# Overflow guard of three attentions: bounds from the weights' Gram matrices in place of peaks of the queries and keys

## The chip, the cores and the metric

The kernel is one program on one core of one Trainium2 chip. The core has five engines with queues of their own: TensorE (PE; its weight loads are listed as PEld), VectorE (DVE), ScalarE (ACT), GpSimd (POOL) and SyncE (SP, which here only issues transfers). The metric is the device time of one execution in microseconds (us); lower is better. A profile is one execution taken by the hardware profiler, and its span runs from the first to the last instruction.

## What is computed

A chain of 16 layers on 4096 tokens of 128 features (16 sequences of 256 tokens), all in float32. Three layers matter here; all are attentions whose softmax the kernel works out without subtracting a row maximum. `x` below is the layer-normed input of the layer.

```
# decay (16 heads of 8)
q = x @ Wq.T + bq;  k = x @ Wk.T + bk
scores = (q . k) * 8**-0.5 * exp(-alpha * |i - j|)
attn = softmax(scores)

# window and sink (16 query heads of 64, 4 key heads)
x = rmsnorm(x, attn_norm_scale)
q = rope(x @ Wq + bq) * 64**-0.25;  k = rope(x @ Wk + bk) * 64**-0.25
scores = where(|i - j| <= 128, q . k, -1e9)
attn = softmax([scores, sink])[..., :-1]

# rope (16 heads of 8; only the real parts are kept)
Q[even] = cos * (x @ Wq + bq)[even] - sin * (x @ Wq + bq)[odd];  K alike
attn = softmax(causal(Q . K / 8**0.5))
```

## The kernel before

The program holds two networks. `Fast` computes every layer and, in softmax, takes exp of the raw scores. That is safe only while no score is large, so `Fast` keeps a table `peaks` of magnitudes, and at its end `over` (L2733) reduces the table to one number for each stage and side (queries, keys), multiplies the two sides, and compares the product with `LIMITS` (L43). If a limit is exceeded, a branch runs `Net`, the same network with row maxima, over everything again. `bad` is a second condition of decay: a negative `alpha`.

Before the change the table is filled with `peak` (L1666): a VectorE `tensor_reduce` that takes the largest magnitude of each partition over one chunk of queries or keys. The tokens are worked in eight chunks of 512 (two sequences).

Decay and rope run in `small_stage` (L2797). Its loop over slots writes every engine's order out by hand: a slot takes one unit of scores (a 128x128 tile of all 16 heads, four matmuls into four PSUM banks), whose exponentials are evicted by ScalarE, or in decay, for the tiles near the diagonal, first multiplied by the decay factors on VectorE (`pt<-ps,dec`). Products with the values follow three slots later, then a copy `raw` of the sums, transposes (`ct,raw`), division, output projection. Banks are of one pool of six, handed out in turn, so a matmul waits for whoever reads the bank of six allocations ago. A list `steps` gives the slot, relative to a chunk's first unit, at which a chunk's other work is issued: projections, masked copies of the queries, and `guard`, at slot 1. In decay a chunk is eight slots; in rope six, with scores taken three units at a time. The steps of the next layer's beginning (`lead`) run beside them; behind decay that is the router of a mixture of experts (`both`, `rank`, `sel`, `idx`), which is mostly small VectorE operations.

Window and sink attention (L3160) has a schedule of its own: 128 units, one a slot; query and key projections in `prepare` at every second slot, their rotation by VectorE (products with cos and sin, a shuffle) and POOL (the sum), peaks four slots later at the end of the slot, the sums of two units' probabilities on POOL (`both`), and four banks for scores and projections.

The rows of the profile name operations by helper: L504 is every matmul (`mm`), L508 every transpose, L528 every ScalarE activation, L531 and L543 VectorE's products, L534 POOL's.

Of the kernel before, what the change touches and what calls it, by code (L numbers as in the profile page):

```python
# [39 lines left out]
BOUND, LOW = 60.0, 38.0  # L40
PEAKS = 4 * NCH
STAGES = DECAY, ROPE, WINDOW, WINDOW1, SINKS, LOCAL_A, LOCAL_B = range(7)
LIMITS = (BOUND * 8**0.5 / 8, BOUND * 8**0.5 / 4, LOW / 64, LOW / 64, LOW, LOW / 8, LOW / 8)  # L43


class Pack:
# [1603 lines left out]
class Fast(Net):  # L1650
# [15 lines left out]
    def peak(self, stage, side, n, ap):  # L1666

        at = (stage * 2 + side) * PEAKS + n
        self.nc.vector.tensor_reduce(self.peaks[:, at : at + 1], ap, AX.XY if len(ap.shape) > 2 else AX.X, ALU.max, apply_absolute_value=True)

    def weights(self, st):

        self.wpool = self.pool(st, "weights", 1)
        self.turns = 0
        self.widths = [max([1] + [self.packs[n].n for n in self.loads[i::2]]) for i in range(2)]
# [1276 lines left out]
    def decay(self, w):  # L2952


        h0 = self.ha
        nc = self.nc
        with ExitStack() as st:
            p1 = self.stage(st, "d1", 1)
            p2 = self.stage(st, "d2", 2)
            na = p1.tile([P, 1], F32, tag="na", name="na")  # L2960
            self.ts(na, w["alpha"], -1.0, ALU.mult)
            dec = p1.tile([P, P], F32, tag="dec", name="dec")
            self.act(dec, w["lag"][:, :P], AF.Exp, scale=na)
            edge = p1.tile([P, T], F32, tag="edge", name="edge")
            self.act(edge, w["edge"], AF.Exp, scale=na)
            bad = p1.tile([P, 1], F32, tag="bad", name="bad")
            self.ts(bad, w["alpha"], 0.0, ALU.is_lt, 1e30, ALU.mult)
            vzs = self.with_ones(p1, 2)

            def evict(kind, pt, ps):  # L2970
                if kind:
                    for r in range(4):
                        self.act(pt[:, r].rearrange("p h t -> p (h t)"), ps[r], AF.Exp, scale=8.0**-0.5)
                    return
                for r in range(4):
                    self.tt(pt[:, r], ps[r].rearrange("p (h t) -> p h t", h=4), dec[:, None, :].broadcast_to([P, 4, P]), ALU.mult)
                flat = pt.rearrange("p r h t -> p (r h t)")
                return lambda: self.act(flat, flat, AF.Exp, scale=8.0**-0.5)

            qs, ks, kxs, qzs, qxs = {}, {}, {}, {}, {}  # L2980

            def project(c):
                for n, held in (("q", qs), ("k", ks)):
                    pq = self.bank("s")
                    self.mm(pq, w["W" + n], h0[:, self.chunk(c)])
                    held[c] = p2.tile([P, CH], F32, tag=n, name=n)
                    self.act(held[c], pq, AF.Identity, bias=w["b" + n])

            def values(c):
                self.values_by_head(w, vzs[c % 2], self.chunk(c))  # L2990

            def queries(c, b):
                qzs[c, b] = self.masked_copy(p1, qs[c], b)

            def keys_by_edge(c):
                kxs[c] = p2.tile([P, CH], F32, tag="kx", name="kx")
                self.gt(self.bt(kxs[c]), self.bt(ks[c]), self.twice(edge), ALU.mult)

            def queries_by_edge(c, b):
                qxs[c, b] = p1.tile([P, 4, T], F32, tag="qx", name="qx", bufs=3)  # L3000
                self.gt(qxs[c, b], qzs[c, b], edge[:, None, :].broadcast_to([P, 4, T]), ALU.mult)

            def guard(c):
                self.guard(DECAY, c, qs[c], ks[c])
                if c == 0:
                    at = DECAY * 2 * PEAKS
                    self.tt(self.peaks[:, at : at + 1], self.peaks[:, at : at + 1], bad, ALU.add)

            def tiles(c, b, it, jt):
                kk, qq = (ks, qzs) if it == jt else (kxs, qxs)  # L3010
                j = b * T + jt * P
                return kk[c][:, j : j + P], qq[c, b][:, :, it * P : it * P + P], vzs[c % 2][:, 2 * b + jt]

            steps = [
                (1, guard), (-6, project), (-5, values), (-4, lambda c: queries(c, 0)), (-3, keys_by_edge),
                (-2, lambda c: queries_by_edge(c, 0)), (0, lambda c: queries(c, 1)), (2, lambda c: queries_by_edge(c, 1)),
            ]
            units = [(0, 0, 0), (0, 1, 1), (1, 1, 0), (1, 0, 1)]
            self.small_stage(w, units, steps, tiles, evict)

    def guard(self, stage, c, q, k):
        self.peak(stage, 0, c, q)
        self.peak(stage, 1, c, k)

    def rope(self, w):
        h0 = self.ha
        nc = self.nc
        with ExitStack() as st:
            p1 = self.stage(st, "o1", 1)
            p2 = self.stage(st, "o2", 2)  # L3030
            vzs = self.with_ones(p1, 2)

            def evict(kind, pt, ps):
                for r in range(4):
                    self.act(pt[:, r].rearrange("p h t -> p (h t)"), ps[r], AF.Exp, scale=8.0**-0.5)
                if kind:
                    p = pt.rearrange("p r h t -> p (r h) t")
                    return lambda: self.tt(p, p, w["causal"][:, None, :].broadcast_to([P, 16, P]), ALU.mult)

            held, qzs = {}, {}  # L3040

            def turned(c, n):
                s = self.chunk(c)
                pe, po = self.bank("s"), self.bank("s")
                self.mm(pe, w[f"W{n}e"], h0[:, s])
                self.mm(po, w[f"W{n}o"], h0[:, s])
                t1 = p2.tile([P, CH], F32, tag=n, name=n)
                t2 = p2.tile([P, CH], F32, tag="t2", name="t2")
                self.stt(self.bt(t1), self.bt(pe), w[f"b{n}e"], self.twice(w["cos"]), ALU.add, ALU.mult)
                self.stt(self.bt(t2), self.bt(po), w[f"b{n}o"], self.twice(w["sin"]), ALU.add, ALU.mult)  # L3050
                self.gt(t1, t1, t2, ALU.subtract)
                held[c, n] = t1

            def values(c):
                self.values_by_head(w, vzs[c % 2], self.chunk(c))

            def queries(c, b):
                qzs[c, b] = self.masked_copy(p1, held[c, "q"], b)

            def tiles(c, b, it, jt):  # L3060
                j = b * T + jt * P
                return held[c, "k"][:, j : j + P], qzs[c, b][:, :, it * P : it * P + P], vzs[c % 2][:, 2 * b + jt]

            steps = [
                (-6, lambda c: turned(c, "q")), (-5, lambda c: turned(c, "k")), (-3, values), (-2, lambda c: queries(c, 0)),
                (0, lambda c: queries(c, 1)), (1, lambda c: self.guard(ROPE, c, held[c, "q"], held[c, "k"])),
            ]
            units = [(0, 0, 1), (1, 0, 0), (1, 1, 1)]
            self.small_stage(w, units, steps, tiles, evict, group=3)
# [90 lines left out]
    def window_attention(self, w, h, n1, ns2):  # L3160
# [3 lines left out]
        with ExitStack() as st:  # L3164
# [28 lines left out]
            def later(slot, f, *args):  # L3193
                due.setdefault(slot, []).append((f, args))

            def prepare(i, step, slot):

                c, side = divmod(i, 2)
                s = self.chunk(c)
                while pending:  # L3200
                    moved()
                if step == 0:
                    qs[i] = p2.tile([P, 4, CH], F32, tag="q", name="q")
                    ks[i] = p2.tile([P, CH], F32, tag="k", name="k")
                    roped("k", side, s, ks[i])
                    later(("last", slot + 4), self.peak, WINDOW + side, 1, c, ks[i])
                for g in ((0,), (1, 2), (3,), ())[step]:
                    roped("q", 4 * side + g, s, qs[i][:, g])
                    later(("last", slot + 4), self.peak, WINDOW + side, 0, 4 * c + g, qs[i][:, g])
                if side == 0 and step > 1:  # L3210
                    pv = self.bank("s")
                    v = p1.tile([P, 2, T], F32, tag="v", name="v", bufs=4)
                    for k in range(2):
                        t = 2 * step - 4 + k
                        self.mm(pv[:, k * T : k * T + T], n1[:, c * CH + t * P : c * CH + t * P + P], w["Wv"])
                        vs[c, t] = v[:, k]
                    self.tt(v, self.bt(pv), w["bv"][:, None, :].broadcast_to([P, 2, T]), ALU.add)
# [626 lines left out]
```

## Time and profile before

| what | us |
|---|---|
| timed runs: lowest, median, highest of 3 | 4231.14, 4233.71, 4234.19 |
| the profiled execution | 4216.97 |
| its span | 4215.2 |
| one peak of 128x512 on VectorE (median of 80 / of 32) | 0.676 / 0.671 |
| their sum (112 of them) | 74.2 |
| stretch of decay, with the end of the layer before | 2160 to 2440 |
| stretch of window and sink attention, without its start | 2900 to 3340 |
| stretch of rope | 3640 to 3840 |

In the timelines a row has the start (us from the start of the span), the time it covers (us), engine, line, operation, tiles written and read, shape, and the count of instructions merged into it; in brackets the idle time of the engine before it and what ended it. A float32 matmul has two records, so `x8` of a full matmul is four matmuls. Rows of one engine can overlap a little, since operations are pipelined.

### The profile page before, as it was taken

How to read it: one execution, taken by the hardware profiler on the slowest of the kernel's cores; microseconds unless marked ns; L12 is line 12 of the kernel's file. 1: busy time of each engine (PE TensorE's matmuls, PEld its weight loads, DVE VectorE, ACT ScalarE, POOL GpSimd, SP SyncE). 2: the span in 40 equal slices, each digit the busy share in tenths (PEclk: the TensorE clock that was granted, in tenths of full speed). 3: DMA queues.
4: the chain of work that ended last, by engine and by line, in shares of the span. 5: the costliest groups of instructions: out<-in, count | busy, mean ns of one | idle time of the engine just before them, and what ended most of it. 6: DMA issues, size and time to landing. Idle time of an engine off the chain costs nothing. (4 is left out here: it accounts for less than half of the span.)

```text
span 4215.2 us, 73089 instructions
## 1 busy us (share of the span) xinstructions
PE 3849.9 (91%) x28742; PEld 2195.1 (52%) x28742; DVE 2557.5 (61%) x4503; ACT 2314.2 (55%) x4485; POOL 1854.9 (44%) x1632
## 2 busy tenths in 40 slices
PE   7999999988899999985989879888999999899878
PEld 3555466465465456554965469543444344455333
DVE  4775576364577377464346633556877677486474
ACT  6666466555766466553456634444555554774532
POOL 4764365232566176326433434454555454321251
PEclk8999999988999999997999979999999999999989
DMA  1800000000000000004920058100000000000000
GB/s 61 345 2 1 11 2 1 20 1 1 20 1 1 3 1 1 1 6 142 320 76 12 16 180 297 41 19 16 1 1 1 3 1 10 6 2 19 6 0 21
DMA packets 78400, 176.38 MB, mean 42 GB/s; under 512 B 12606, under 2 KB 39108, under 8 KB 77920
## 3 DMA queue, kind: packets, MB, share of 16 engines
q1 hardware_dynamic: 65568, 148.40, 10.2%
q0 software_dynamic: 9120, 18.51, 1.3%
q8 instruction: 229, 3.75, 0.4%
q10 hardware_dynamic: 3360, 4.72, 0.4%
q14 instruction: 123, 1.01, 0.1%
HBM read 118.28 MB, written 54.20 MB: 41 GB/s over the span
## 5 line engine op out<-in xcount | busy, mean ns | idle before, releaser
L528 ACT ACTIVATE pt<-ps 128x512 f32<-128x512 f32 x640 | 339.9, 600 | 327.6 <-PE ps L504 326.4
L504 PE MATMUL ps<-hb,w 128*128 128x512 f32 (+1 forms) x960 | 461.0, 613 | 3.7 <-issue 3.3
L504 PE MATMUL ps<-w,hb 128*128 128x512 f32 (+2 forms) x896 | 403.8, 572 | 23.5 <-DVE t L531 18.6
L534 POOL TENSOR_TENSOR t<-t,t 128x512 f32<-128x512 f32 x256 | 319.8, 1271 | 161.1 <-DVE t L531 140.6
L531 DVE TENSOR_TENSOR t<-ps,tab 128x512 f32<-128x512 f32 x512 | 317.7, 682 | 84.6 <-ACT sq L528 81.1
L534 POOL TENSOR_TENSOR t<-t,ss 128x1024 f32<-128x1024 f32 x128 | 243.7, 1904 | 192.8 <-ACT ss L528 191.6
L504 PEld LDWEIGHTS ps<-hb,w 128*128 128x128 f32 (+1 forms) x960 | 178.6, 190 | 259.6 <-issue 223.0
L528 ACT ACTIVATE qkt<-ps 128x512 f32<-128x512 f32 x256 | 140.5, 595 | 291.7 <-PE ps L508 291.7
L531 DVE TENSOR_TENSOR u<-u,ps 128x384 f32<-128x384 f32 (+1 forms) x206 | 121.8, 596 | 288.0 <-PE ps L508 186.4
L531 DVE TENSOR_TENSOR ot<-ps,rd 128x512 f32<-128x512 f32 (+2 forms) x224 | 143.3, 640 | 203.2 <-ACT rd L528 203.2
L534 POOL TENSOR_TENSOR nsq<-ha 128x512 f32<-128x512 f32 x112 | 123.5, 1103 | 320.6 <-ACT ha L528 308.6
L504 PEld LDWEIGHTS ps<-w,hb 128*128 128x128 f32 x896 | 157.1, 194 | 178.6 <-issue 125.5
L534 POOL TENSOR_TENSOR both<-pt 128x1024 f32<-128x1024 f32 x64 | 151.2, 2363 | 199.8 <-DVE pt L531 164.1
L504 PE MATMUL ps<-nsq,ct 128*128 128x512 f32 x368 | 203.1, 635 | 34.3 <-POOL nsq L534 30.4
L504 PE MATMUL ps<-ot,w 128*128 128x512 f32 x448 | 213.2, 610 | 17.7 <-DVE ot L531 9.8
L504 PE MATMUL ps<-xt,w 128*128 128x128 f32 x1704 | 221.3, 281 | 1.5 <-ACT xt L528 1.5
L2199 POOL DMA_INDIRECT back<-y,x x142 | 139.1, 980 | 184.1 <-DVE y L538 63.3
L504 PE MATMUL ps<-u,w 128*128 128x512 f32 (+1 forms) x448 | 215.4, 605 | 3.5 <-POOL u L534 3.5
L504 PEld LDWEIGHTS ps<-xt,w 128*128 128x128 f32 x1704 | 205.2, 195 | 2.9 <-ACT xt L528 2.9
L528 ACT ACTIVATE u<-ps,w 128x512 f32<-128x512 f32 x160 | 107.8, 685 | 179.6 <-PE ps L504 177.0
L528 ACT ACTIVATE nrs<-ps,ct 128x512 f32<-128x512 f32 x208 | 139.7, 683 | 103.4 <-PE ps L504 97.8
L3741 POOL DMA_INDIRECT rows<-out,idx x128 | 126.1, 985 | 155.0 <-ACT out L528 105.5
(362 smaller groups left out, 8880.2 us busy)
## 6 DMA issues: line engine op xcount, KB each, us to landing
w<-in_moe_x SPq DMA_DIRECT2D x142, 533.0 KB
rows<-t SPq DMA_DIRECT2D x64, 520.0 KB
x<-rows SPq DMA_DIRECT2D x142, 65.0 KB
w<-in_local_f SPq DMA_DIRECT2D x8, 659.5 KB
y<-back ACTq DMA_DIRECT2D x16, 256.0 KB
y<-back SPq DMA_DIRECT2D x16, 256.0 KB
w<-in_local_f SPq DMA_DIRECT2D x4, 658.5 KB
back<-y,x POOLq DMA_INDIRECT x142
```

The costliest lines, as they stand in the source:

```text
L504: self.nc.tensor.matmul(out, lhsT, rhs, start=start, stop=stop)
L528: self.nc.scalar.activation(out, in_, func, **kw)
L531: self.nc.vector.tensor_tensor(out, a, b, op)
L534: self.nc.gpsimd.tensor_tensor(out, a, b, op)
L2199: nc.gpsimd.indirect_dma_start(views[i], bass.IndirectOffsetOnAxis(ap=x[:, C : C + 1].bitcast(I32), axis=0), y, None, bounds_check=2 * NT ...
L3741: nc.gpsimd.indirect_dma_start(views[(c * 2 + k) * 4 + t], bass.IndirectOffsetOnAxis(ap=idx[:, k, t : t + 1], axis=0), out[:, k, t], None,)
```

## The change

The table is no longer filled from queries and keys but, once in each stage, from the weights. For a weight matrix W with columns of outputs, `norm_bound` has TensorE compute the Gram matrix W^T W (in window attention with the squared norm scale between, which POOL multiplies into a copy of W first), VectorE sums the magnitudes of each of its rows, and the largest sum bounds the square of the largest stretching of W. In decay only the 8x8 blocks of the heads are kept (one more VectorE product). A second matmul gives the squared length of the bias. `over` is unchanged, so the products compared with the limits are now of squared lengths, and the limits of decay, rope and both window sides are rewritten for that. The limits of the other stages and the sinks' peak stay.

All of it is issued in chunk 1 of each stage: decay at slot 1 of the chunk (two matrices), rope at slot 1 (four matrices: even and odd parts of Wq and Wk), window attention at the place of the old peak of the keys, once a side (four matrices of Wq, one of Wk). The 16 peaks of decay, 16 of rope and 80 of window attention are gone.

```diff
-LIMITS = (BOUND * 8**0.5 / 8, BOUND * 8**0.5 / 4, LOW / 64, LOW / 64, LOW, LOW / 8, LOW / 8)
+LIMITS = (BOUND**2 * 8, BOUND**2 * 8, (LOW * 8) ** 2, (LOW * 8) ** 2, LOW, LOW / 8, LOW / 8)
...
+    def norm_bound(self, pool, bank, stage, side, mats, biases, scaled=None, times=1.0, block=False):
+
+        n = len(mats)
+        at = (stage * 2 + side) * PEAKS
+        pg, pb = self.bank(bank), self.bank(bank)
+        for i, (m, b) in enumerate(zip(mats, biases)):
+            self.mm(pg[:, i * P : i * P + P], m, scaled[i] if scaled else m)
+            self.mm(pb[:, i : i + 1], b.broadcast_to([P, P]), b)
+        gram = pg[:, : n * P].rearrange("p (m d) -> p m d", d=P)
+        if block:
+            t = pool.tile([P, n, P], F32, tag="gram", name="gram", bufs=1)
+            self.tt(t, gram, self.k["blk8"][:, None].broadcast_to([P, n, P]), ALU.mult)
+            gram = t
+        r = pool.tile([P, n], F32, tag="bound", name="bound", bufs=1)
+        self.nc.vector.tensor_reduce(r, gram, AX.X, ALU.add, apply_absolute_value=True)
+        self.ts(r, r, P * times * 16.0 / 15.0, ALU.mult)
+        self.stt(self.peaks[:, at : at + n], pb[:, :n], 16.0 * times, r, ALU.mult, ALU.add)
...
             def guard(c):
-                self.guard(DECAY, c, qs[c], ks[c])
-                if c == 0:
+                if c == 1:
+                    for side, n in enumerate("qk"):
+                        self.norm_bound(p1, "s", DECAY, side, [w["W" + n]], [w["b" + n]], block=True)
                     at = DECAY * 2 * PEAKS
                     self.tt(self.peaks[:, at : at + 1], self.peaks[:, at : at + 1], bad, ALU.add)
...
-    def guard(self, stage, c, q, k):
-        self.peak(stage, 0, c, q)
-        self.peak(stage, 1, c, k)
...
+            def guard(c):
+                if c == 1:
+                    for side, n in enumerate("qk"):
+                        mats, biases = ([w[k + n + part] for part in "eo"] for k in "Wb")
+                        self.norm_bound(p1, "s", ROPE, side, mats, biases, times=2.0)
...
-                (0, lambda c: queries(c, 1)), (1, lambda c: self.guard(ROPE, c, held[c, "q"], held[c, "k"])),
+                (0, lambda c: queries(c, 1)), (1, guard),
...
+            def guard(side):
+                for k, n in enumerate("qk"):
+                    tiles = range(4 * side, 4 * side + 4) if n == "q" else (side,)
+                    mats = [w["W" + n][:, g * P : g * P + P] for g in tiles]
+                    scaled = p1.tile([P, 4, P], F32, tag="scaled", name="scaled")
+                    for i, m in enumerate(mats):
+                        nc.gpsimd.tensor_scalar(scaled[:, i], m, w["ns1"], w["ns1"], ALU.mult, ALU.mult)
+                    self.norm_bound(
+                        p1, "s", WINDOW + side, k, mats, [w["b" + n][:, g : g + 1] for g in tiles],
+                        [scaled[:, i] for i in range(len(mats))],
+                    )
...
-                    later(("last", slot + 4), self.peak, WINDOW + side, 1, c, ks[i])
+                    if c == 1:
+                        later(("last", slot + 4), guard, side)
                 for g in ((0,), (1, 2), (3,), ())[step]:
                     roped("q", 4 * side + g, s, qs[i][:, g])
-                    later(("last", slot + 4), self.peak, WINDOW + side, 0, 4 * c + g, qs[i][:, g])
```

## The prediction

> **What bounds the kernel now.** The page first, for the share of each engine, then the busy time of the three stages that the change touches (decay, window and sink attention, rope).
>
> ```profile
> PE 3849.9 (91%) x28742; PEld 2195.1 (52%) x28742; DVE 2557.5 (61%) x4503; ACT 2314.2 (55%) x4485; POOL 1854.9 (44%) x1632
> ```
>
> ```profile
> 2160.00:2440.00 280.00, 251.48 (x2938) 138.98 (x2936) 181.50 (x421) 191.97 (x299) 103.62 (x80) 0.94 0.04 13
> ...
> 2900.00:3340.00 440.00, 438.93 (x3374) 179.06 (x3376) 350.08 (x550) 230.04 (x505) 242.22 (x138) 1.00 0.00 1
> ...
> 3640.00:3840.00 200.00, 191.85 (x2266) 111.10 (x2264) 162.03 (x219) 140.77 (x284) 38.51 (x31) 0.97 0.01 4
> ```
>
> The columns are the stretch, its length, busy time of PE, PEld, DVE, ACT and POOL, then the clock granted. TensorE is full in the window stage (438.9 of 440.0) and nearly so in rope (191.9 of 200.0); decay alone has 28.5 us of idle TensorE. So VectorE time taken out of window or rope is worth nothing in the steady state, and TensorE time put in costs its full length. Next, what is taken out:
>
> ```profile
> L1669 DVE TENSOR_REDUCE peaks<-q x80: 668/676/686, 2173.3 to 3816.7; 128x1 f32<-128x512 f32 x80
> L1669 DVE TENSOR_REDUCE peaks<-k x32: 668/671/678, 2173.9 to 3817.3; 128x1 f32<-128x512 f32 x32
> ```
>
> Two of them, overlapping, hold VectorE's queue for 1.19 us (2265.01 to 2266.19 below). Where they matter is seen in the timelines of VectorE and TensorE in decay's fourth chunk.
>
> ```profile
> 2265.01 0.68 DVE L1669 TENSOR_REDUCE peaks<-q 128x1 f32<-128x512 f32 x1
> 2265.60 0.68 DVE L1669 TENSOR_REDUCE peaks<-k 128x1 f32<-128x512 f32 x1
> 2266.19 2.48 DVE L531 TENSOR_TENSOR pt<-ps,dec 128x512 f32<-128x512 f32 x4
> ...
> 2271.48 0.68 DVE L639 COPY raw<-ps 128x512 f32<-128x512 f32 x1
> ```
>
> ```profile
> 2264.14 1.08 PE L2866 MATMUL ps<-pt,vo 128*32 128x128 f32 x32
> 2265.15 1.99 PE L504 MATMUL ps<-ha,w 128*128 128x512 f32 x4
> 2267.06 2.78 PE L504 MATMUL ps<-qx,kx 32*128 32x512 f32 x8
> 2270.24 0.19 PE L504 MATMUL ps<-both,before 128*128 128x32 bf16 x1 [0.40 <-DVE both L538]
> ...
> 2272.31 0.81 PE L508 MATMUL ps<-ct,raw 128*128 128x128 f32 x4 [1.71 <-ACT pt L528]
> 2273.05 1.94 PE L2866 MATMUL ps<-pt,vo 128*32 128x128 f32 x32
> 2274.91 1.68 PE L504 MATMUL ps<-w,ha 128*128 128x128 f32 x8
> ```
>
> From 2265 to 2273 VectorE has no gap: the two peaks, the decay products, the router's small operations, the copy `raw`. TensorE's scores (qx,kx) stretch to 2.78 us waiting for banks, and then it waits 1.71 us. The row names ACT, but `raw` ends at 2272.16 and the transposes read it at 2272.31; in the last chunk the same wait is put down to `raw` itself. Here VectorE decides.
>
> **The change, part by part.**
>
> *Taken out of decay, chunks 2 to 7* (the router of the following stage runs beside these): 1.19 us of a VectorE chain that TensorE waits for, six times: **-7.1 us**. Bounds: 0, if what comes next (ScalarE's exponentials, which end at 2272.28) holds TensorE instead; -7.1. I take the full value, because the wait ends on `raw`. Chunk 0: 0; there the peaks and the addition of `bad` hold VectorE from 2173.30 to 2175.98, but TensorE runs slow score matmuls to 2177.48 and waits for ScalarE's banks (bounds 0 and -2.7).
>
> *Taken out of rope and window:* hidden behind the full TensorE, but for the start of the window stage, shown in the timelines of VectorE, POOL and TensorE:
>
> ```profile
> 2890.98 0.67 DVE L1669 TENSOR_REDUCE peaks<-k 128x1 f32<-128x512 f32 x1
> 2891.57 0.67 DVE L1669 TENSOR_REDUCE peaks<-q 128x1 f32<-128x512 f32 x1
> ...
> 2895.32 1.26 DVE L1669 TENSOR_REDUCE peaks<-q 128x1 f32<-128x512 f32 x2
> ```
>
> ```profile
> 2898.63 2.08 PE L504 MATMUL ps<-q,k 64*128 64x512 f32 x4 [7.63 <-POOL q L534]
> ```
>
> The first scores wait for POOL's last rotated query, which waits for VectorE; four peaks stand in that chain: 2 x 1.2 = **-2.4 us** (bounds 0, -2.4).
>
> *Added in decay, once, in chunk 1:* two Gram matmuls and two bias matmuls on TensorE, eight short VectorE operations. Four 128x128 matmuls (w,ha, x8 records) took 1.08 us at 2182.91, so a Gram matrix is 0.27; the nearest row to a bias matmul (one column) is the router's 128x8, four in 0.89, so 0.22. Two pairs: 1.0 us. VectorE's chain (product 0.28, reduction 0.2, two of 0.17, all twice) is 1.7 us where the two peaks were 1.2; the next scores need two of the banks that it frees. In chunk 1 TensorE had no gap, so **+1.1** (bounds 0 and +2.0, when both are paid).
>
> *Added in rope, once, in chunk 1:* four pairs, 2.0 us of TensorE. More is in the banks: with four banks taken by the guard, the next scores have to use the two of the key projections just before. Those are read by VectorE at 3677.24 and 3677.90, after a mask product that runs from 3675.03; then the guard's own reduction has to be done (0.4 and twice 0.17). So the scores that began at 3675.49 and ended at 3676.6 now end near 3680.1: **+3.5** (bounds 2.0, the matmuls alone; 5.0, with a clock loss as below).
>
> *Added in the window stage, twice, in chunk 1:* five pairs each, 2.45 us of TensorE, and five scalings of 128x128 weights by POOL, for which the Gram matmuls wait. POOL stands behind `both`; TensorE in program order right behind the scores:
>
> ```profile
> 2939.11 2.36 POOL L534 TENSOR_TENSOR both<-pt 128x1024 f32<-128x1024 f32 x1 [1.25 <-DVE pt L531]
> ```
>
> ```profile
> 2938.34 1.13 PE L504 MATMUL ps<-q,k 64*128 64x512 f32 x4
> 2939.40 1.12 PE L504 MATMUL ps<-hb,w 128*128 128x512 f32 x2
> ```
>
> The guard sits where hb,w begins, at 2939.40; `both` ends at 2941.46. Up to 2.06 us of stall for side 0, and for side 1 up to 0.69 (2968.15 against 2968.84). Without peaks VectorE feeds `both` earlier; I take 1.2 and 0.5. A scaling has no row here; POOL's 128x128 products are 0.45 to 0.62 us and its 128x1024 tensor-scalar 1.08 (an eighth is 0.14). I take 0.4, nearer the rows of its size. The keys' scaling uses the same buffer, so it waits until the fourth Gram matrix is done: 0.4 and a handover of 0.2. Sum: 1.7 stalls + 2 x 0.4 + 2 x 2.45 + 2 x 0.6 = 8.6 us. Queued behind: all of TensorE; on VectorE the shuffles behind the guard's reductions; on POOL the rotations of q. These have slack of some us, as the scores that need them come four units later. No DMA is added or moved, and SP's and POOL's transfer queues are unchanged.
>
> *The clock.* At 2273.05 the same 32 matmuls that took 1.08 us at 2264.14 took 1.94, and w,ha 1.68 against 1.08: after 2.3 us with almost nothing on TensorE its rate is halved, which costs 0.15 + 0.86 + 0.60 = 1.6 us. A guard in the window stage is such a stretch: a stall, then matmuls that are mostly weight loads. I take one such loss for the two guards: +1.5 (bounds 0, +3.0). So window is **+10.1** (bounds 4.9, the matmuls alone; 13.5, with stalls of 2.06 and 0.69, scalings of 0.62 and both clock losses).
>
> The Trainium skill ("TensorE: Matmul & The Clock Gate", section "HAM oscillation — how this bites in real kernels") has the clock fall only after an idle gap of more than about 3.4 us. By it no guard would lose the 1.5 us and the sum would be +3.7; the 1.94 us row, behind two gaps of 0.40 and 1.71, says that less suffices, and I go by the row.
>
> Sum: -7.1 + 1.1 + 3.5 - 2.4 + 10.1 = **+5.2 us**. The profiled execution took 4216.97 us (its span 4215.2); the timed median is 4233.71, 16.7 us more. The difference is put on the median: 4239 us.
>
> **The rivals.**
>
> *The guards cost more than decay gives back.* The rate is halved after all four guards (4 x 1.5 instead of 1.5: +4.5), and only half of decay's 7.1 us arrives, as ScalarE ends at 2272.28 in any case (+3.6): 5.2 + 8.1 = +13.3, 4247 us. For it: ScalarE's end so near to TensorE's start. Against: the last chunk's wait names `raw`.
>
> *Not slower: decay gives back twice.* One mechanism, in decay's chunks 2 to 7: the empty stretch there shrinks below what halves the rate, so each chunk saves 1.6 us besides the 1.19. Losses elsewhere are 1.1 + 3.5 + 10.1 - 2.4 = 12.3 us, so it decides from 12.3 / 6 = 2.05 us per chunk. At 2.79 the sum is -4.4, 4229 us. Against: scores and `raw` both move up by 1.2, so the stretch between them stays.
>
> *The bounds are too coarse and the slow second program runs too.* A limit exceeded runs the whole network again: more than twice the span, over 8400 us. From the inputs' weights I work out the products of the bounds as 8222 (decay) and 9967 (rope) against 28800, and 8040 and 7305 (window) against 92416. Nothing trips.
>
> **How the numbers follow.** Forecast 0.50, first rival 0.34, second 0.15, third 0.01. What can be told from no change is about 0.2%, 8.5 us. The forecast lies within it but for its upper edge (0.45 same, 0.05 slower); the first rival is slower (0.33) and at its edge the same (0.01); the second is the same (0.05) or, where the window guards are hidden as well, faster (0.10). So faster 0.10, same 0.51, slower 0.39. Range: all lower bounds give -7.1 - 2.7 - 2.4 + 0 + 4.9 + 2.0 = -5.3, all upper ones +2.0 + 5.0 + 13.5 = +20.5; I go from -5.7 to +18.3, 4228 to 4252. The forecast's own range, with each step off by about a quarter of its bounds, is 4233 to 4244.
>
> **What would show it.** Decay's stretch (from its first scores to the end of its last `raw`) shorter by some 6 us; the first window scores 2.4 us nearer to the start of the stage; TensorE idle for about 1 us before the first Gram matrix of each side, and 4 to 5 us from there to the next hb,w; in rope the scores behind the guard at over 2 us instead of 1.14. Wrong, if decay's chunks keep their 34 to 38 us, if POOL's scalings take over 1 us each, or if TensorE shows half-rate matmuls behind every guard.

## The result and the profile after

After the change the median is 4243.55 us (4236.12 to 4249.32), beside 4235.83 for the kernel before on the same chip: a ratio of 1.0017, 95% interval 1.0011 to 1.0024, or +7.2 us (4.7 to 10.2). The forecast was 4239, from a difference of +5.2. The profiled execution took 4242.21 us, its span is 4240.3. On the page, the engines' busy time:

```profile
PE 3857.1 (91%) x28806; PEld 2200.5 (52%) x28806; DVE 2497.8 (59%) x4417; ACT 2314.9 (55%) x4485; POOL 1858.6 (44%) x1642
```

VectorE is 59.7 us less busy and TensorE 7.2 us more, with 64 more matmul records; the kernel is slower all the same. The places that the prediction named, one after the other. TensorE's timeline in decay, at the stretch shown of before from 2265.15 on:

```profile
2281.28 1.98 PE L504 MATMUL ps<-ha,w 128*128 128x512 f32 x4
2283.20 1.59 PE L504 MATMUL ps<-qx,kx 32*128 32x512 f32 x8
2285.19 0.19 PE L504 MATMUL ps<-both,before 128*128 128x32 bf16 x1 [0.40 <-DVE both L538]
...
2287.26 1.09 PE L508 MATMUL ps<-ct,raw 128*128 128x128 f32 x4 [1.71 <-DVE at L531]
2288.27 1.94 PE L2884 MATMUL ps<-pt,vo 128*32 128x128 f32 x32
2290.14 2.08 PE L504 MATMUL ps<-w,ha 128*128 128x128 f32 x8
```

The scores (qx,kx) take 1.59 us where they took 2.78: the 1.19 us of the two peaks have gone. The two gaps (0.40 and 1.71) and the slow matmuls behind them (1.94, 2.08) have not. In the window stage, the first scores and the guard of side 0:

```profile
2906.34 2.08 PE L504 MATMUL ps<-q,k 64*128 64x512 f32 x4 [5.27 <-POOL q L534]
```

```profile
2945.70 1.13 PE L504 MATMUL ps<-q,k 64*128 64x512 f32 x4
2948.81 0.49 PE L504 MATMUL ps<-scaled,w 128*128 128x128 f32 x2 [1.98 <-POOL scaled L3223]
2949.13 0.28 PE L504 MATMUL ps<-w 128*128 128x1 f32 x2
...
2951.24 0.49 PE L504 MATMUL ps<-scaled,w 128*128 128x128 f32 x2 [0.49 <-POOL scaled L3223]
2951.57 0.28 PE L504 MATMUL ps<-w 128*128 128x1 f32 x2
2951.71 1.73 PE L504 MATMUL ps<-hb,w 128*128 128x512 f32 x2
2953.24 1.91 PE L504 MATMUL ps<-w,hb 128*128 128x256 f32 x4
```

The first scores wait 5.27 us, 2.36 less than before (7.63). At the guard, TensorE stands still for 1.98 us until POOL has scaled the first weights, works through four pairs, stands still for another 0.49 for the keys, and then hb,w takes 1.73 us (1.12 before). In rope:

```profile
3694.08 1.84 PE L504 MATMUL ps<-w 128*128 128x128 f32 x16
3696.72 2.11 PE L504 MATMUL ps<-qz,k 32*128 32x512 f32 x6 [0.80 <-DVE k L543]
3699.01 1.55 PE L504 MATMUL ps<-qz,k 32*128 32x512 f32 x2 [0.19 <-DVE peaks L543]
3700.49 4.02 PE L2884 MATMUL ps<-pt,vo 128*32 128x128 f32 x96
```

The same scores and weighing before, and TensorE in two steps of the clock after (columns as in the prediction: stretch, length, busy time of PE, PEld, DVE, ACT and POOL, then the granted clock):

```profile
3675.49 1.19 PE L504 MATMUL ps<-qz,k 32*128 32x512 f32 x8
3676.61 2.83 PE L2866 MATMUL ps<-pt,vo 128*32 128x128 f32 x96
```

```profile
3696.16:3699.57 3.41, 2.67 (x8) 1.17 (x8) 3.12 (x7) 1.64 (x3) 1.27 (x1) 1.00 0.00 0
3699.57:3702.99 3.42, 3.42 (x50) 2.33 (x52) 0.29 (x2) 1.08 (x3) 0.00 (x0) 0.50 0.02 5
```

Four pairs come first, then scores that wait for banks (3.66 us; 1.19 before), most of that at a granted clock of 1.00, and then one step at half rate, in which the weighing is slow (4.02; 2.83 before).

### The profile page after: what moved, and what is told of

Its sections match the earlier page's. It is cut to its first block, busy times and chain, and to the rows that moved or that the text cites. A ratio compares the mean times of both kernels' runs of the same rounds, so it can differ in the third digit from the quotient of the medians.

```text
span 4240.3 us, 73220 instructions
## 1 busy us (share of the span) xinstructions
PE 3857.1 (91%) x28806; PEld 2200.5 (52%) x28806; DVE 2497.8 (59%) x4417; ACT 2314.9 (55%) x4485; POOL 1858.6 (44%) x1642
## 3 DMA queue, kind: packets, MB, share of 16 engines
q1 hardware_dynamic: 65568, 148.40, 10.1%
q14 instruction: 123, 1.01, 0.1%
## 5 line engine op out<-in xcount | busy, mean ns | idle before, releaser
L534 POOL TENSOR_TENSOR t<-t,ss 128x1024 f32<-128x1024 f32 x128 | 243.7, 1904 | 193.0 <-ACT ss L528 191.8
L504 PE MATMUL ps<-ot,w 128*128 128x512 f32 x448 | 213.4, 611 | 17.7 <-DVE ot L531 9.8
```

Source lines behind the costliest of these rows:

```text
L504: self.nc.tensor.matmul(out, lhsT, rhs, start=start, stop=stop)
L534: self.nc.gpsimd.tensor_tensor(out, a, b, op)
```

## The experiments

Every comparison is with the kernel before on the same chip. Chips differ: before took 4234.23 us in the first series and 4213.21, 4214.88 and 4213.64 in the other three, so times of different series are not set against each other, only ratios (turned into us below).

**One stage alone, and no guard at all.** From the changed kernel, the old `peak` calls and limits are put back in two of the three stages; in the fourth kernel all guards of the three are left out.

```
# decay_only: rope and window go back, likewise rope_only and window_only
-                if c == 1:
-                    for side, n in enumerate("qk"):
...
-                        self.norm_bound(p1, "s", ROPE, side, mats, biases, times=2.0)
+                self.peak(ROPE, 0, c, held[c, "q"])
+                self.peak(ROPE, 1, c, held[c, "k"])
# no_guards: neither norm_bound nor peak in the three stages
```

> Decay alone has the bound from the Gram matrices; rope and the window stage keep their peaks. Theory A (the prediction): six chunks give 1.19 us each and the one guard costs 1.1 to 1.6, so the kernel is 5.5 to 6 us faster than before, about 4230 against 4236. Rival B: the stretches of TensorE at half rate between the decay chunks take it back, as in the one profile of the change, where decay came out 0.8 to 1.6 us longer; then the difference is -1 to +2 us. In the trace, A and B agree on the stretch from the turned output to the scores (half of it or less at half rate, 1.2 us shorter); they differ on decay's length from its first score to its last: 6 us shorter in A, within 2 us of before in B.

> Rope alone has the bound; decay and the window stage keep their peaks. The prediction's term is +3.5 us for the one guard in chunk 1, and nothing for the peaks that go. Rival: as the profile of the change reads, +6.4 us, because the matmuls that follow run at half the rate. In the trace: from ha,w ahead of the guard to the next scores but one, 5.7 us before, 9.2 by the prediction, 12.1 by the rival. If the peaks that go give something back elsewhere in rope, the whole comes out lower than the length of that place says.

> The window stage alone has the bound; decay and rope keep their peaks. By the prediction -2.4 us at its start and +10.1 for two guards: +7.7 us. Rival: as the profile of the change reads, -2.4 and +12.6 (6.6 for the first side, 6.0 for the second): +10.2 us, half of it from TensorE at half rate behind each guard. In the trace: from the score ahead of the guard to the next weighing, 4.0 us before, 9.1 by the prediction, 10.6 by the rival.

> Neither peaks nor bounds in decay, rope and the window stage (the overflow guard of these three stages is left out). This is what the change could give if its own guards were free. Theory A (the prediction): decay -7.1 and the window's start -2.4, together -9.5 us, about 4226. Rival B: decay's return is eaten by half-rate stretches, which leaves -2.4 and the decay guard's absence, -2 to -4 us. Rival C: the peaks also cost something in rope or in the later window slots, which no term of the prediction has; then more than 11 us.

Measured: decay alone -6.8 us (-10.2 to -3.0), rope alone +6.8 (3.0 to 10.6), window alone +11.0 (6.4 to 15.7), none -10.6 (-15.2 to -5.9). So decay does give back what was forecast; rope and window cost what the profile of the change showed, more than forecast; and free guards would have been worth 10.6 us.

**Where the window's and rope's cost comes from, and the guards at another place.** `window_early` keeps the Gram matmuls where they are and issues all ten scalings (`scale`) ahead of the slots; `rope_split` does the queries in chunk 1 and the keys in chunk 2; `starts` moves every guard ahead of the first scores (chunk 0, slot -1).

```
# window_early (window stage only)
+            scales = p1.tile([P, 10, P], F32, tag="scaled", name="scaled")
...
+                scale()
                 for n in range(-14, len(units) + 16):
# rope_split (rope only)
-                if c == 1:
-                    for side, n in enumerate("qk"):
+                if c in (1, 2):
+                    side, n = c - 1, "qk"[c - 1]
# starts (all stages; the same for decay), and scale() as above
-                (0, lambda c: queries(c, 1)), (1, guard),
+                (-1, guard), (0, lambda c: queries(c, 1)),
...
+                    if n == 0:
+                        guard(0, "o")
+                        guard(1, "o")
```

> The window stage alone has the bound, at the same places as in the change, but all ten scalings are issued on POOL ahead of the stage into buffers of their own; decay and rope keep their peaks. This takes away the stall ahead of the Gram matmuls and the turnaround of the keys (1.98 + 0.49 and 1.39 + 0.49 us idle) and leaves the matmuls. Theory A: the idle time brings on the half rate; both go, and each side costs its five pairs, 2.3 us; whole -2.4 + 4.6 = +2.2 us, and hb,w behind the guard takes 0.95. Rival B: the small matmuls bring it on; hb,w behind the guard still takes 1.7 to 2.0, each side costs 2.3 + 1.9 us, whole +6.

> Rope alone has the bound, with the queries' part in chunk 1 and the keys' part in chunk 2, so that each place holds two pairs of matmuls and two banks; decay and the window stage keep their peaks. Theory A: the wait for banks and the half rate behind the guard come from four pairs at once; then each place costs 0.9 us and the whole is +1.8 us instead of +6.4. Rival B: each place loses its wait and its half rate again, 3 us or more each: +6 us or more. Decay has its peaks here: if its length from the first scores to the last ranks is 309 us as in two of three such profiles, and not 298 as in the profile of before, the profile of before caught a short one.

> All three stages have the bounds, but computed ahead of the first scores of each stage, where TensorE stands still in the trace (3.0 us in decay, 4.5 in rope, 5.3 in the window stage), with the ten scalings issued on POOL before the window stage's first chunk. Theory A: the guards then cost about nothing, and what is left is decay's return and the window's start: -8 to -10.6 us, about 4225, as without guards. Rival B: the half-rate stretches behind the guards come with the small matmuls wherever they stand, and each delays the first scores: 0 to -5 us.

`window_early` came out at +2.1 us (-1.7 to 5.9). TensorE behind the same five pairs:

```profile
2936.45 0.47 PE L504 MATMUL ps<-scaled,w 128*128 128x128 f32 x2
2936.75 0.28 PE L504 MATMUL ps<-w 128*128 128x1 f32 x2
2937.25 1.12 PE L504 MATMUL ps<-hb,w 128*128 128x512 f32 x2 [0.22 <-DVE bound L1685]
2938.21 1.03 PE L504 MATMUL ps<-w,hb 128*128 128x256 f32 x4
```

The matmuls are the same, the stalls are gone, and hb,w is back at 1.12. So in the window stage the small matmuls alone do not bring on the slow rate; without the idle time it stays away, and the pairs cost no more than their own time.

`rope_split` is at +8.0 us (4.2 to 11.8): theory A fell. Its place in chunk 1:

```profile
3675.46 0.95 PE L504 MATMUL ps<-w 128*128 128x128 f32 x8
3676.33 1.13 PE L504 MATMUL ps<-qz,k 32*128 32x512 f32 x4
3678.08 2.52 PE L504 MATMUL ps<-qz,k 32*128 32x512 f32 x4 [0.62 <-DVE k L543]
3680.54 5.35 PE L2884 MATMUL ps<-pt,vo 128*32 128x128 f32 x96
```

Two pairs and two banks are enough: the scores still have to take a bank that VectorE reads late (`k`), two steps at half rate follow (3678.98 to 3685.81), and the weighing takes 5.35 us. In chunk 2 the keys' two pairs cost 2.3 us (8.0 from ha,w to the next scores but one, where 5.7 were): the scores take 2.72 us, but no half rate follows, and the weighing takes its 2.83. So four pairs at once are not needed for the loss, and half rate does not come at every such place.

`starts` is at -8.8 us (-12.6 to -5.1), with one wait left: a Gram matmul of the second side stands 3.09 us for a bank that VectorE frees late.

```profile
2880.19 0.46 PE L504 MATMUL ps<-scaled,w 128*128 128x128 f32 x2 [3.09 <-DVE bound L1685]
```

**The last causes.** `starts2` takes that wait away. `filled` is the kernel before with work for TensorE in decay's two gaps. `rope_late` moves rope's guard two slots.

```
# starts2: keys' Gram matrix beside the biases, two banks a side
+                    dst = pb[:, P : 2 * P] if n == "k" else pg[:, i * P : i * P + P]
# filled (place, in decay): results that nobody reads
+                net.mm(pp[:, 64:], h0[:, s.start : s.start + P], h0[:, s.start + 64 : s.stop])
...
+                net.mm(pf, h0[:, s.start : s.start + P], h0[:, s])
+                net.mm(pf[:, :T], h0[:, s.start : s.start + P], h0[:, s.start : s.start + T])
# rope_late
-                (0, lambda c: queries(c, 1)), (1, guard),
+                (0, lambda c: queries(c, 1)), (3, guard),
```

> As the kernel with all bounds ahead of the first scores of the stages, but the window stage's keys share a bank with the biases, so that the four banks of the weighed sums hold both sides and no Gram matmul waits for a bank (3.09 us in that kernel, which put its first window scores some 3 us later than in the kernel with early scalings). Theory: -8.9 - 2.9 = -11 to -12 us against before, as much as without guards (-10.6). Rival: the first scores wait for the rotated queries anyway, and the bank wait cost nothing: -9 again.

> The kernel before, with its peaks, and two idle stretches of TensorE per decay chunk filled with matmuls whose results nobody reads: one of 448 columns ahead of the sorting's matmuls, one of 512 and one of 256 behind them, together some 2.2 us of work in gaps of 1.6 and 1.6 us. Theory: the half rate in decay comes from too little work in a step of 3.41 us, so it stays away from these stretches; six to eight stretches that cost 1.7 us each go, against up to 0.6 us each of added work: -4 to -10 us, and under 35 us of half rate in decay instead of 58 to 65. Rival: the rate isn't set by TensorE's work, or the added work costs as much: 0 to +8 us.

> Rope alone has the bound, in chunk 1 but two slots later than in the change, behind the values' projection and not right behind the turned keys; decay and the window stage keep their peaks. Theory A: the four pairs of matmuls cost 1.8 us, and the wait for banks that VectorE reads late (0.8 to 1.0 us) is what brings on the half rate (3.6 us of the 6.4); without it +2 to +3. Rival B: the small matmuls bring on the half rate wherever they stand: +5 to +6.5.

`rope_late`: 0.0 us (-3.8 to 3.8); the pairs' own 1.8 us lie within the interval. The same 16 records, with no idle time behind them, the clock at 1.00 throughout, and scores of 1.91 us where the kernel before has 1.99 at this place:

```profile
3676.68 1.84 PE L504 MATMUL ps<-w 128*128 128x128 f32 x16
3678.45 1.91 PE L504 MATMUL ps<-qz,k 32*128 32x512 f32 x8
...
3682.29 2.83 PE L2884 MATMUL ps<-pt,vo 128*32 128x128 f32 x96
```

So in rope, too, it was the place, right behind the keys' projection whose banks VectorE reads last, and not the work.

`filled`: -12.2 us (-17.7 to -7.2), although TensorE does more. The windows of TensorE on a grid of 3.41 us show why. The columns are as in the prediction: stretch, length, busy time of PE, PEld, DVE, ACT and POOL, and the granted clock. First the kernel before at the stretch quoted there, then `filled` at the same work:

```profile
2265.81:2269.22 3.41, 3.41 (x11) 1.42 (x10) 3.41 (x7) 2.37 (x4) 0.00 (x0) 1.00 0.00 0
2269.22:2272.64 3.42, 1.31 (x14) 0.63 (x12) 3.04 (x17) 3.06 (x4) 0.00 (x0) 1.00 0.00 0
2272.64:2276.05 3.41, 3.41 (x40) 2.61 (x39) 0.86 (x4) 0.00 (x0) 0.00 (x0) 0.50 0.00 0
2276.05:2279.46 3.41, 3.41 (x53) 2.16 (x52) 2.47 (x4) 1.17 (x3) 0.30 (x1) 1.00 0.02 5
```

```profile
2262.48:2265.89 3.41, 3.41 (x12) 1.41 (x12) 3.19 (x11) 3.05 (x6) 0.00 (x0) 1.00 0.00 0
2265.89:2269.30 3.41, 3.41 (x50) 2.25 (x49) 2.66 (x13) 1.61 (x1) 0.00 (x0) 1.00 0.00 0
```

Before, one step with 1.31 us of work is followed by exactly one step at a clock of 0.50. With the gaps filled no step falls below 1.00. All of decay has 54.2 us of half rate before and 28.0 in `filled`. (`filled` also takes one bank more in each chunk, which moves the waits for banks; what that alone does was not measured.) Behind the half rate at the start of the stage, `filled` has its next such step at 2405.86, 243.7 us into decay; before has five by then.

`starts2` gave -19.0 us (-24.9 to -13.5), more than either theory. In its trace the first scores of the window stage come 4.1 us earlier than in `starts`, of which 3 were expected, and decay is 8.9 us shorter than before's. Some 5 us of the 19 are not placed; only five timed runs stand behind it.

**Both mends together, and the change once more.**

> The last kernel with all bounds ahead of the first scores (keys sharing a bank with the biases) and the two filled stretches of each decay chunk together. Theory: the two gains add up but for the peaks' return, since without peaks and with filled gaps the sorting's end in each chunk still waits for VectorE: -19 and half of -12, about -22 to -28 us against before. Rival: the filling took away the same half-rate stretches that the peaks' going took away: -19 us, no more.

> The changed kernel itself, beside the others on the same chip. +5 to +10 us against before by what was measured. What it tells apart: decay's length from its first scores to the last ranks, in a profile from a chip where the kernel before takes 298 us for it in four of four profiles. Theory: 298 less 6 us, 290 to 293. Rival (half rate takes the return back): 296 to 300, as in the first profile of the change.

`starts_filled` (the code of `starts2` with the two lines of `filled`): 4191.80 us against 4213.64, -20.6 (-26.5 to -15.2), the best of all. Whether the two gains add up is not told apart by the times: the interval holds both the -22 of the theory and the -19 of its rival. In decay's length they do: it is 9.9 us shorter than in `starts2` and 9.5 shorter than in `filled`. The change itself on that chip: 4224.38, +12.6 (8.0 to 16.9). Its decay takes 291.9 us against 298.1 to 298.4 in the kernels with peaks on the two chips with about the same time for before, so the return is there.

The stages' lengths in all profiles, in us, worked out from the traces (decay: from its edge factors on ScalarE to the last ranks; start: from the sinks' exponential to the first window scores; window: from there to the last reciprocal; rope: from its first scores to its last weighing):

| kernel | decay | start | window | rope |
|---|---|---|---|---|
| before | 298.1 | 25.0 | 445.5 | 187.2 |
| after | 299.1 | 21.3 | 457.8 | 191.6 |
| first series: decay_only | 300.7 | 23.7 | 445.4 | 185.3 |
| rope_only | 309.3 | 23.7 | 445.4 | 191.6 |
| window_only | 310.3 | 21.3 | 457.6 | 185.2 |
| no_guards | 295.2 | 21.4 | 445.5 | 187.2 |
| other series: window_early | 298.1 | 22.7 | 450.2 | 185.2 |
| rope_split | 298.4 | 25.1 | 445.5 | 196.0 |
| starts | 285.3 | 25.6 | 444.4 | 186.8 |
| starts2 | 289.2 | 21.5 | 444.5 | 187.0 |
| filled | 288.8 | 23.7 | 445.6 | 187.3 |
| rope_late | 298.1 | 25.1 | 445.5 | 186.9 |
| starts_filled | 279.3 | 21.5 | 442.9 | 186.9 |
| after_again | 291.9 | 21.3 | 457.3 | 194.3 |

The table shows a trap. By the first two rows decay gives nothing back (298.1, 299.1). But the same code with peaks takes 309.3 and 310.3 us on the first series' chip and 298.1 to 298.4 on the others, and the kernels before and after need not have been profiled on like chips. That the chip is the reason is not shown: each kernel was profiled once. Within the first series the bounds are 9.1 us shorter (300.7 against 309.8), within the others 6.2 (291.9 against 298.1). Even so a length is good to some 4 us only: `starts` and `starts2` have the same code in decay and take 285.3 and 289.2 us, and `no_guards` has a decay 14.6 us shorter than with peaks, more than the whole kernel gained (10.6; 5.9 to 15.2).

Where decay's return comes from is seen from one chunk's ranks (`rank<-ahead`) to the next's. The first number is the interval, the second the half rate in it, in us:

| kernel | 1 to 2 | 2 to 3 | 3 to 4 | 4 to 5 | 5 to 6 | 6 to 7 | 7 to 8 |
|---|---|---|---|---|---|---|---|
| before | 34.2, 3.4 | 37.5, 3.4 | 37.7, 3.4 | 37.7, 3.4 | 34.2, 3.4 | 28.0, 10.7 | 19.7, 16.3 |
| after_again | 33.0, 3.4 | 36.3, 3.4 | 37.7, 6.8 | 34.9, 0 | 31.4, 0 | 28.1, 9.9 | 20.8, 20.8 |
| filled | 32.6, 0 | 36.0, 0 | 36.1, 0 | 36.1, 0 | 32.7, 0 | 26.5, 4.8 | 19.8, 13.0 |
| starts_filled | 31.5, 0 | 34.8, 0 | 34.9, 0 | 34.9, 0 | 31.5, 0 | 25.6, 0 | 18.1, 7.7 |

Where the half rate is equal, an interval without peaks is 1.1 to 1.2 us shorter (the first two of `after_again` against before, the first five of `starts_filled` against `filled`). A step of half rate more or less moves it by 1.2 to 1.6 us besides: the third interval of `after_again` returns nothing, the fourth and fifth 2.8 each.

## Why the prediction was right, and where it was not

The forecast (within 4228 to 4252, no change that can be told) held, because its terms and their signs held; two of them were sized too small, and decay's sum came out right in part by luck. On the last series' chip the difference is +12.6 us, more than the 8.5 that the forecast took for no change, and its interval does not hold the +5.2. Point by point:

- *Decay, -7.1 + 1.1.* The mechanism is right: 1.1 to 1.2 us come back in an interval whose half rate stays as it was. "Six times" is not what happened: by the table of intervals the return is 1.2, 1.2, 0.0, 2.8, 2.8, nothing and a loss of 1.1. From the first ranks to the last that makes -6.8 (`after_again` 222.2 us, `rope_late` 229.0), near the forecast -7.1 because half-rate steps won and lost, which have no term, and chunks without return nearly cancel. The guard itself was put low: the first ranks come 69.7 us into the stage with it and 68.1 without peaks or guard, so 1.6. Against it stand the first chunks' peaks, which were put at nothing and give 1.0 back (69.1 with peaks, 68.1 without).
- *Window's start, -2.4.* Right: 23.7 to 21.3 (from 25.1 in other profiles).
- *Window guards, +10.1.* Measured +12 (445.5 to 457.3, 457.6 and 457.8). Stalls with the first scaling were put at 2.5 and are 1.98 + 1.39, 0.9 more; ten pairs at 4.9 are 4.8; the keys' turnaround at 1.2 is 1.0. The step that was mis-sized is "I take one such loss for the two guards: +1.5". There is one behind each, 2.9 us together (3.37 and 3.32 us for two matmuls that took 1.9).
- *Rope guard, +3.5.* The term that was mis-sized most, outside its own upper bound of 5.0: in the profile of the change +6.4 (12.1 us from ha,w to the next scores but one, where 5.7 were). Matmuls were put at 2.0 and took 1.84. The wait is the one that it named, for banks that VectorE reads behind its mask product and in the guard, but it was put at 1.5 and is some 3.0: 0.99 idle, the rest inside the scores' rows. Their four matmuls start within 0.07 us of each other before (3675.49 to 3675.56) and one by one after (3696.72, 3697.37, 3697.70, 3699.01), each 0.05 to 0.06 us behind the end of the VectorE operation that frees its bank. VectorE's three guard operations, put at 0.74 us, took 1.72 (3697.24 to 3698.96). The half rate, one step, cost the remaining 1.6; the sum had none here, and the bound had 1.5.
- *The clock.* "After 2.3 us with almost nothing on TensorE its rate is halved" was right as a row and wrong as a rule. In rope 0.80 and 0.19 us of idle time went before half rate, and in two chunks of decay in `after_again` the same gaps of 0.40 and 1.71 us are followed by full rate:

```profile
2341.99 0.19 PE L504 MATMUL ps<-both,before 128*128 128x32 bf16 x1 [0.40 <-DVE both L538]
...
2344.05 0.63 PE L508 MATMUL ps<-ct,raw 128*128 128x128 f32 x4 [1.71 <-DVE at L531]
2344.61 1.08 PE L2884 MATMUL ps<-pt,vo 128*32 128x128 f32 x32
```

```profile
2339.58:2342.99 3.41, 2.37 (x18) 0.86 (x16) 3.10 (x13) 2.88 (x6) 0.00 (x0) 1.00 0.00 0
2342.99:2346.41 3.42, 2.36 (x43) 2.02 (x44) 2.08 (x11) 2.08 (x2) 0.00 (x0) 1.00 0.00 0
2346.41:2349.82 3.41, 3.41 (x53) 2.17 (x53) 2.64 (x5) 1.35 (x4) 0.47 (x1) 1.00 0.02 5
```

Here a step of the clock ends inside the longer gap, so that two steps share the idle time, with 2.37 and 2.36 us of work; before, one step had both gaps and 1.31. To go by the row and not by a gap of 3.4 us was right for the guards, since no gap there is that long and half rate follows all the same. (The loss read from the rows is 1.5 us and not 1.6: w,ha at 2182.91 covers 1.16 us, and 1.08 is the distance to the next row.)
- *The rivals.* The first (guards cost more) had the better eye for the guards: half rate did follow those of window and rope, though not decay's. Its other half, that decay returns only half, fell with `decay_only`. The second needed empty stretches to shrink; they stayed 0.40 and 1.71 us. Even so two intervals of `after_again` returned the 2.8 us that it reckoned with, since their stretches lie elsewhere on the clock's grid, and another lost as much as a step. `filled` shows the size of what it was after, by added work and not by peaks that go.

By `after_again` and `rope_late` (for rope, where `rope_late` has the bound itself, the kernel before) the stages sum to -6.2 - 3.8 + 11.8 + 7.1 = +8.9 us, inside the measured +7.2 (4.7 to 10.2) and +12.6 (8.0 to 16.9).

## What to carry to other kernels

Work that runs once should be issued where the engine that it needs stands still anyway, ahead of a stage's first scores: the same bounds made the kernel 7.2 and 12.6 us slower inside chunk 1 and 8.8 and 19.0 us faster there. Before small matmuls are put into a full stretch, look at what they wait for and whose banks they take, since here the matmuls' own 7.6 us (4.8 in the window stage, 1.8 in rope, 1.0 in decay) cost less than the waits (3.4 + 1.0 in the window stage, 3.0 in rope) and the half rate behind them (2.9 and 1.6), 11.9 us together. A wait for a bank can stand inside a row of matmuls and not ahead of it. And compare stages only between profiles of one chip, and not to the last 4 us.

## What the runs showed of the hardware

**The clock is granted in steps of 3.41 us on a fixed grid.** In all fourteen traces, every edge between 1.00 and 0.50 falls on a grid of 3.413 us, to 0.01 us, and half rate lasts a whole number of steps (3.4, 6.8, 10.2 us). With each trace from 2160 to 4190 us cut on its own grid, for before, after and `starts` together, the step's busy share and the clock of the next step are:

| step | busy share | next step full | next step half |
|---|---|---|---|
| full rate | under 0.45 | 3 | 51 |
| full rate | 0.45 to 0.70 | 75 | 14 |
| full rate | 0.70 and more | 1462 | 8 |
| half rate | under 0.85 | 2 | 73 |
| half rate | 0.85 and more | 71 | 19 |

So a step that is busy for less than 0.45 is nearly always followed by half rate, and half rate nearly always lasts until a step is almost full. The same wait can cost a step of half rate or none, then, by what else stands in its step, as decay's gaps did above. Busy time is not all that counts: the step with side 0's Gram matmuls was busy for 2.74 of 3.41 us, and the one in rope's guard for 2.67, and half rate followed both, while the step just ahead of side 0's, with 1.62, was followed by full rate.

```profile
2945.21:2948.63 3.42, 1.62 (x16) 0.38 (x8) 1.19 (x2) 1.68 (x5) 2.66 (x2) 1.00 0.00 0
2948.63:2952.04 3.41, 2.74 (x21) 2.60 (x22) 1.12 (x4) 0.34 (x1) 1.88 (x5) 1.00 0.00 0
2952.04:2955.45 3.41, 3.41 (x8) 1.73 (x8) 3.00 (x9) 0.00 (x0) 1.68 (x2) 0.50 0.01 2
```

What the chip measures there is not shown. The Trainium skill ("TensorE: Matmul & The Clock Gate", section "What's actually happening") has a free-running window of 3413 ns that sets the clock to one of two rates; the grid of 3.413 us and the clocks of 1.00 and 0.50 agree. It lists the half rate behind an idle window, though, and here a window with 1.31 us of work was enough.

**A tiny VectorE operation can wait for a whole POOL instruction.** In rope's guard on VectorE and POOL:

```profile
3697.68 1.00 DVE L538 TENSOR_SCALAR bound<-bound 128x2 f32<-128x2 f32 x1
...
3699.53 0.17 DVE L538 TENSOR_SCALAR bound<-bound 128x2 f32<-128x2 f32 x1
```

```profile
3697.40 1.27 POOL L534 TENSOR_TENSOR k<-k,t 128x512 f32<-128x512 f32 x1 [3.75 <-DVE t L543]
```

The first of two equal operations began inside POOL's sum and ended with it (3698.68 and 3698.67), 0.83 us late; the last of the four score matmuls stood behind it (3699.01). It takes 1.00 or 1.01 us in every trace in which it falls beside that sum (`after_again`, `rope_only` and both times in `rope_split`), and 0.17 in `rope_late`, where it does not. Not every such operation is held: one of 128x1 took 0.15 us inside a POOL product in `starts` (at 2165.49). The Trainium skill ("SBUF — State Buffer", section "SBUF: two separate sides") describes one port pair that VectorE, in some of its operations, shares with POOL and that is held for a whole instruction, which fits these rows. POOL's scaling of 128x128 took 0.45 us, close to the 0.4 that the prediction took.
